# A six-stage decoder block on one core: the second cross attention issued in text order on four engines

## The chip, the cores and the metric

One core of a Trainium2 chip runs the whole program. The metric is device microseconds of one execution, a median over several. PE is TensorE's matmul, PEld its weight load, DVE is VectorE, ACT ScalarE, POOL GpSimd, SP SyncE, which here issues nearly all DMAs. `L1361` is line 1361 of the kernel before.

## The reference

Two layers on `x` of 4 batches x 256 tokens x 256 features, with a context of 1601 keys for each batch. Six stages add to `x`: self attention, a first cross attention to the context ("memory attention"), a ternary feed forward, a recurrence, the second cross attention, and a mixture of 8 experts of which each token uses 2. Each stage starts from the layer norm of `x`. The change is about the second cross attention and the experts, which share its time:

```python
q = _rms_norm((x @ Wq.T).reshape(b, 256, 16, 128), q_norm_w)
kv_in = concatenate([context, x], axis=1)            # 1857 keys
k = _rms_norm((kv_in @ Wk.T).reshape(b, 1857, 4, 128), k_norm_w)
v = (kv_in @ Wv.T).reshape(b, 1857, 4, 128)
q, k = _rope(q, positions_of_queries), _rope(k, positions_of_keys)
k, v = repeat(k, 4), repeat(v, 4)                    # 4 key heads serve 16 query heads
attn = softmax(q @ k.T / sqrt(128)) @ v
x = x + attn.reshape(b, 256, 2048) @ Wo.T

logits = layernorm(x) @ w_gate                       # 8 experts, the best 2 weighted
x = x + sum(weight * (silu(y @ wi_0[e]) * (y @ wi_1[e])) @ wo[e])
```

## The kernel before

All matrices are float32. Keys are handled in 15 chunks of 128 (the last has 65). A *head* is one of the 16 combinations of batch `b` and key head `g`; each has two *pairs* of query heads, so 32 pairs. A pair is worked through in 8 *steps* of two chunks:

- `score` (L1361 to L1366): on PE scores of a chunk for 512 queries (two heads x 256), `bsc`; ACT copies them, scaled by the key's factor `kn`, into a tile `s` of the ring of 12; DVE keeps the running maximum `acc`. ACT and DVE read the same PSUM bank, and DVE waits for ACT's copy.
- `maximum` (L1373 to L1379): after the last chunk PE transposes `acc` (`tm`), DVE reduces it to `mq`, and a half step or more later PE spreads `mq` over all partitions (`bc`).
- `exponential` (L1383 to L1398), ten steps after the score (`DE`): DVE subtracts `bc`, ACT takes the exponential, POOL adds the two halves to the row sums `sum`.
- `weigh` (L1407), eleven steps after the score (`DW`): PE multiplies by the values into `bpo`.
- `finish` (L1413 to L1441): ACT copies `bpo` to `aT`, PE adds up the sums over keys (`ts`), DVE inverts them, PE projects with `wo` (`bpw`), DVE adds the result to `x`.

`steps` (L1531) runs step `s` as: exponential of chunk pair `s-10`, score `s`, `others(2s)`, weigh `s-11`, `others(2s+1)`. The table `places` holds, for each *place* (half step), pieces of generators that prepare other work: `put(place, gen, last, bank)` enters one piece, and with `bank` moves on to the next place if the place already holds a piece that wants a bank. While head `k-1` is scored, from place `base = 32 (k-1)` on, head `k` is prepared:

- `prep_q` (L1229): `pq` on PE, ACT's squares, DVE's two products with cosine and sine tables (`rotate`), POOL's addition and its power -1/2 of the sum of squares (`factor`, L1196 to L1199), all in one piece; five places later ACT scales by the factor (`normed`, L1203); eight places after the first piece PE transposes (`tpq`) and ACT copies to `qT`.
- `prep_kv` (L1258), four units `i` of up to four chunks, at places 22, 26, 30 and 34 of `base`: projection `pk`, rotate and factor in one piece, eight places later the transposes `tpk` and ACT's copy to `kT` (L1303).
- for the first head of a batch also `angles` (nine pieces on DVE, the last with two sines on ACT, L1142 to L1144), `tokens` (layer norm of `x`, inverse root by `rsqrt`, whose power runs on POOL at L272) and `tables` (L1160 to L1165: four products on DVE for the keys, four for the queries, two to a piece; the keys' at places 7 and 11 of `base`).
- `tiles` (L1205), called by the first preparation, also issues the four loads of the values that the start of the program left in DRAM.

`experts(b)` of an earlier batch goes through the same table, in 23 pieces: seven of routing, then for each expert one piece of `mph` on PE, tanh on ACT and two products on DVE, and one of `mpe` on PE and DVE's addition to `x`. Three experts of batch 2 are kept for the end (`KEPT`), beside batch 3's.

PSUM tiles come from `p1`, a ring of six banks; `bc` and `bpo` have one each. SBUF tiles of 128x1024 for context, expert weights and raw keys come from `db`, three buffers.

The text only fixes dependencies and a priority: the framework's scheduler, which works with its own estimates of durations, puts the instructions of each engine into a fixed order, and each engine then runs its list in that order. The lists of all engines, SP's included, are made that way before. The first eight steps are entered while the last stages of batch 3 are still going; `run(work)` (L1596) enters all later ones.

Of the kernel before, what the change touches and what calls it, by code (L numbers as in the profile page):

```python
# [20 lines left out]
P = 128  # L21
# [95 lines left out]
def decoder_kernel(ctx: ExitStack, tc: tile.TileContext, at, t, out):  # L117
# [861 lines left out]
    def experts(b):  # L979
# [13 lines left out]
        r1 = rsqrt(mv[:, :, 1], 1e-5, f"mo{b}")  # L993
# [31 lines left out]
        V.tensor_sub(w2, tops[1], tops[0])  # L1025
        A.activation(w2, w2, AF.Exp)
# [13 lines left out]
        def inner(e):  # L1040
# [17 lines left out]
            A.activation(it, ph[:, 0:256], AF.Tanh, scale=0.5)  # L1058
            V.scalar_tensor_tensor(it, it, 1.0, ph[:, 0:256], ALU.add, ALU.mult)
# [18 lines left out]
        for e in range(NE + ahead):  # L1078
            if e < NE:
                its.append(inner(e))  # L1080
                if not final:
                    yield
            if e >= ahead:
                outer(e - ahead, its[e - ahead])
            yield
# [61 lines left out]

    def tables(b, only="kq"):

        d = bt[b]  # L1150
        ang, sn = d["angles"]
        for nm, n, w in (("k", NCH, knw), ("q", 2, qnw)):
            if nm not in only:
                continue
            tb = [P, n, 64]
            ctab = wk.tile([P, n, HD1], F32, tag=f"c{nm}", name=f"ctab{nm}{b}")
            stab = wk.tile([P, n, HD1], F32, tag=f"s{nm}", name=f"stab{nm}{b}")
            wlo, whi = w[:, None, 0:64].to_broadcast(tb), w[:, None, 64:128].to_broadcast(tb)
            d[nm] = (ctab, stab)
            V.tensor_mul(ctab[:, :, 0:64], ang[:, 0:n, :], wlo)  # L1160
            V.tensor_mul(ctab[:, :, 64:128], ang[:, 0:n, :], whi)
            yield

            V.scalar_tensor_tensor(stab[:, :, 64:128], sn[:, 0:n, :], -1.0, whi, ALU.mult, ALU.mult)
            V.tensor_mul(stab[:, :, 0:64], sn[:, 0:n, :], wlo)  # L1165
            yield

    def normed_tokens(b):
        mv = moments(xs[b], f"xb{b}")
        r1 = rsqrt(mv[:, :, 1], 1e-5, f"xb{b}")  # L1170
        bt[b]["centred"] = lambda: centred(fa(0, f"bxh{b}"), xs[b], mv, r1)
# [14 lines left out]
    def rotate(src, ctab, stab, sq, r, u):  # L1186


        A.activation(sq[:, :, 0:HD1], src, AF.Square)
        V.tensor_mul(r, src, ctab)  # L1190
        V.tensor_mul(u, src, stab)  # L1191
# [13 lines left out]
    def tiles(b, g):  # L1205

        if (b, g) not in gt:
# [11 lines left out]
            for i in range(4):  # L1219
                if (b, i) in kept_values:  # L1220
                    n, w = units(i)
                    r = min(P, w)
                    nc.sync.dma_start(
                        out=gt[b, g]["v"][0:r, 4 * i + 2 : 4 * i + 2 + n, :],
                        in_=kept_values[b, i][:, 0:r, g * HD1 : (g + 1) * HD1].rearrange("c p n -> p c n"),
                    )
        return gt[b, g]

    def prep_q(b, g, j):  # L1229
# [10 lines left out]
        ctab, stab = (a[:, j : j + 1, :].to_broadcast([P, 4, HD1]) for a in d["q"])  # L1240
# [3 lines left out]
        rotate(pq.rearrange("p (h d) -> p h d", h=4), ctab, stab, sq, r, u)  # L1244
        factor(sq, r, u, 4, nm, rn)
# [12 lines left out]
    def prep_kv(b, g, i):  # L1258
# [17 lines left out]
        if done:  # L1276
            o = n - done
            ctab, stab = (a[:, 4 * i + o : 4 * i + n, :] for a in d["k"])
            rotate(raw, ctab, stab, *(a[:, o:n, :] for a in (sq, r, u)))
        for h in range(0, n - done, 2):  # L1280
# [10 lines left out]
            ctab, stab = (a[:, 4 * i + h : 4 * i + h + m, :] for a in d["k"])  # L1291
# [4 lines left out]

        factor(sq, r, u, n, nm, e["kn"][:, 4 * i : 4 * i + n])
# [7 lines left out]
    def before_head(b, g):  # L1305

        if g == 0:
            if b == 0:
                yield from angles(b)
            yield from tables(b)  # L1310
        late = None
        for i in (1, 2, 3):
            gen = prep_kv(b, g, i)
            next(gen)
# [13 lines left out]
        for gen in (prep_q(b, g, 0), prep_q(b, g, 1), prep_kv(b, g, 0)):  # L1328
            next(gen)
# [125 lines left out]
    QA, KA, HB, HC = (2, 6), (11, 13, 15, 17), 5, 8  # L1455
# [37 lines left out]
    for k, (b, g) in enumerate(heads):  # L1493
        base = 32 * (k - 1)
        if k:
            if g == 0:
                gen = angles(b)
                for i in range(9):
                    put(base - 81 + 6 * i, gen, i == 8)
                gen = tokens(b)  # L1500
                for i, o in enumerate((-8, -6, -3)):
                    put(base + o, gen, i == 2, i == 2)
                for o, n in ((-5, "q"), (-3, "q"), (7, "k"), (11, "k")):
                    gen = tables(b, n) if o in (-5, 7) else gen
                    put(base + o, gen, o in (-3, 11))
            for f, when in ((prep_q, QA), (prep_kv, KA)):
                for i, o in enumerate(when):
                    gen = f(b, g, i)
                    spot = put(base + 2 * o, gen, bank=f is prep_q)
                    if f is prep_q:  # L1510
                        put(spot + HB, gen)
                    put(spot + HC, gen, True, True)
        gen = loader(b, g)
        put(base + 60, gen, True)
    for b in range(B - 1):
# [3 lines left out]
        pieces = 23 if b < B - 2 else 23 - 2 * KEPT  # L1519
        for i in range(pieces):  # L1520
            spot = put(spot, gen, i == 22, i not in (0, 1, 2, 5, 6)) + (5 if i > 6 else 3)
# [74 lines left out]
    run(work)  # L1596
    assert not places, sorted(places)
    gen = experts(B - 1)
    for _ in range(KEPT):
        next(gen)  # L1600
        next(kept)
        next(kept)
# [67 lines left out]
```

## Time and profile before

| what | value |
|---|---|
| median of 3 runs (lowest to highest) | 1747.34 us (1746.52 to 1749.41) |
| profiled execution, device time | 1749.43 us |
| its span, first to last instruction | 1747.4 us |
| mean granted TensorE clock | 0.993 |
| first score to last weighing | about 510 to 1709 us |
| POOL `sum` (L1398), 411 | 536.7 us, 1306 ns each |
| PE `bsc` (L1361) and `bpo` (L1407), 960 each | 459.5 and 459.9 us |
| ACT `s` (L1362), 480; `s` (L1386), 256 | 316.5 and 256.5 us |
| DVE `acc` (L1366), 448; `s` (L1383), 256 | 333.0 and 289.4 us |

A float32 matmul stands in the profile as two PE instructions, so a chunk's score of 128x512 counts two. Where a row of a group says `idle before <- releaser`, the engine stood still before these instructions and the releaser is what it waited for. In a list by order of time, the columns are start, duration from the first to the end of the last, engine, line, operation and tiles, how many are merged, and in brackets idle time before it. In a list by stretches, the columns are the stretch, its length, the busy time of each engine, the granted clock, the DMA share and GB/s.

### The profile page before, as it was taken

What the parts mean: (1) busy time and instruction counts of PE and PEld (TensorE: products, weight loads), DVE (VectorE), ACT (ScalarE), POOL (GpSimd) and SP (SyncE); (2) the same over time, 40 slices, a digit from 0 to 9 for tenths busy, and PEclk for the clock granted to TensorE, in tenths of its full rate; (3) what the DMA queues carried; (4) which work ended last, traced back from release to release, by engine and by line L of the source; (5) the groups of instructions that cost most, each with busy time, mean ns of one, the idle gap of its engine ahead of it and who ended that gap; (6) DMA issues with size and microseconds to landing.
All of it is one profiled execution on the core that took longest, in us unless ns stands there. A gap on an engine that the chain in (4) does not pass through costs nothing.

```text
span 1747.4 us, 20643 instructions
## 1 busy us (share of the span) xinstructions
PE 1694.9 (97%) x6642; PEld 971.5 (56%) x6642; DVE 1302.7 (75%) x2429; ACT 997.4 (57%) x1742; POOL 877.5 (50%) x719
## 2 busy tenths in 40 slices
PE   8899989999999999999999999999999999999998
PEld 4455668765555455554555555555555555445546
DVE  6653476787668777787877878777877878788776
ACT  3456653656456656566665656556565656656551
POOL 2210032211126576676766756655665776676651
PEclk9999999999999999999999999999999999999999
DMA  7221334212231121121212121121222113011102
GB/s 258 99 90 50 90 99 128 75 66 90 97 109 46 38 82 35 55 58 31 89 32 70 47 67 52 55 82 35 73 61 67 51 37 93 26 37 48 43 0 67
DMA packets 113554, 119.10 MB, mean 68 GB/s; under 512 B 10000, under 2 KB 87332, under 8 KB 113448
## 3 DMA queue, kind: packets, MB, share of 16 engines
q1 hardware_dynamic: 111624, 116.39, 21.6%
q10 hardware_dynamic: 1824, 1.41, 0.3%
q8 instruction: 53, 0.87, 0.2%
q14 instruction: 53, 0.43, 0.1%
HBM read 100.20 MB, written 17.57 MB: 67 GB/s over the span
## 4 chain that ended last, share of the span: by engine, by line
PE 64%; DVE 12%; POOL 9%; ACT 9%; issue 4%; DMA 1%; POOLq 0%; DVEq 0%; ACTq 0%
PE bpo L1407 17%; PE bsc L1361 16%; PE pk L1290 5%; POOL sum L1398 5%; PE mph L1053 2%; PE bpw L1437 2%; PE vah L355 2%; ACT s L1386 2%; ACT s L1362 2%; DVE acc L1366 1%; PE xpo L740 1%; DVE s L1383 1%; PE pq L1239 1%; POOL ropeq L1196 1%; PE xsc L695 1%
## 5 line engine op out<-in xcount | busy, mean ns | idle before, releaser
L1398 POOL TENSOR_TENSOR sum<-sum,s 128x512 f32<-128x512 f32 (+1 forms) x411 | 536.7, 1306 | 84.1 <-ACT s L1386 59.0
L1361 PE MATMUL bsc<-qTb,kTb 128*128 128x512 f32 (+1 forms) x960 | 459.5, 599 | 6.8 <-ACT kTb L1303 6.7
L1407 PE MATMUL bpo<-s,vb 128*128 128x512 f32 (+1 forms) x960 | 459.9, 598 | 0.4 <-ACT s L1386 0.4
L1362 ACT ACTIVATE s<-bsc,kn 128x512 f32<-128x512 f32 (+1 forms) x480 | 316.5, 683 | 211.6 <-PE bsc L1361 194.6
L1366 DVE SCALAR_TENSOR_TENSOR acc<-bsc,kn,acc 128x512 f32<-128x512 f32 x448 | 333.0, 743 | 89.2 <-ACT s L1362 73.3
L1383 DVE TENSOR_TENSOR s<-s,bc 128x1024 f32<-128x1024 f32 (+1 forms) x256 | 289.4, 1142 | 14.7 <-PE bc L1379 14.5
L1386 ACT ACTIVATE s<-s 128x1024 f32<-128x1024 f32 (+1 forms) x256 | 256.5, 1006 | 53.8 <-DVE s L1383 52.2
L1361 PEld LDWEIGHTS bsc<-qTb,kTb 128*128 128x128 f32 (+1 forms) x960 | 174.2, 188 | 191.9 <-issue 135.3
L1407 PEld LDWEIGHTS bpo<-s,vb 128*128 128x128 f32 (+1 forms) x960 | 169.8, 191 | 141.7 <-issue 137.9
L1389 POOL TENSOR_TENSOR sum<-s 128x512 f32<-128x512 f32 x32 | 40.8, 1276 | 198.6 <-ACT s L1386 198.6
L1196 POOL TENSOR_TENSOR ropek<-ropek,ropuk 128x512 f32<-128x512 f32 (+1 forms) x64 | 78.2, 1222 | 123.7 <-DVE ropuk L1191 122.4
L1203 ACT ACTIVATE ropeq<-ropeq,rnq 128x128 f32<-128x128 f32 x128 | 41.2, 390 | 110.7 <-POOL rnq L1199 107.1
L355 PE MATMUL vah<-wv,vcT 128*128 128x512 f32 (+1 forms) x156 | 77.7, 633 | 5.1 <-DMA vcT<-in_ctxT 3.1
L1290 PEld LDWEIGHTS pk<-wkv,cTk 128*128 128x128 f32 x624 | 76.3, 192 | 8.3 <-issue 4.5
L1290 PE MATMUL pk<-wkv,cTk 128*128 128x128 f32 x624 | 77.4, 275 | 0.0
L1199 POOL TENSOR_TENSOR kn<-ssk,nhalf 128x4 f32<-128x4 f32 (+1 forms) x64 | 66.2, 1034 | 17.5 <-DVE ssk L1198 15.0
L1364 DVE TENSOR_SCALAR acc<-bsc,kn 128x512 f32<-128x512 f32 x32 | 24.0, 750 | 59.7 <-ACT s L1362 59.7
L1437 PEld LDWEIGHTS bpw<-wo,aT 128*128 128x128 f32 x256 | 48.5, 190 | 34.8 <-issue 21.1
L272 POOL TENSOR_TENSOR rsr_xa<-rse_xa,nhalf 128x2 f32<-128x2 f32 x4 | 3.4, 854 | 126.0 <-DVE rse_xa L270 126.0
L1437 PE MATMUL bpw<-wo,aT 128*128 128x256 f32 x256 | 65.6, 379 | 0.3 <-ACT aT L1413 0.3
L1196 POOL TENSOR_TENSOR ropeq<-ropeq,ropuq 128x512 f32<-128x512 f32 x32 | 43.8, 1368 | 40.2 <-PE bsc L1361 17.8
L358 ACT COPY vst<-vah 128x512 f32<-128x512 f32 (+1 forms) x52 | 30.2, 591 | 56.0 <-issue 18.3
(509 smaller groups left out, 2589.7 us busy)
## 6 DMA issues: line engine op xcount, KB each, us to landing
v<-vst SPq DMA_DIRECT2D x48, 256.0 KB
vb<-v SPq DMA_DIRECT2D x48, 256.0 KB
cTk<-in_ctxT SPq DMA_DIRECT2D x24, 512.0 KB
wq<-in_wq SPq DMA_DIRECT2D x16, 512.0 KB
wo<-in_wo SPq DMA_DIRECT2D x16, 512.0 KB
wi<-in_wi SPq DMA_DIRECT2D x32, 256.0 KB
xcT<-in_ctxT SPq DMA_DIRECT2D x12, 512.0 KB
xct<-in_ctx SPq DMA_DIRECT2D x12, 512.0 KB
```

The lines of the kernel that those rows point to most:

```text
L355: T.matmul(pv[0:r, :], lhsT=cT[:, c, k * P : k * P + r], rhs=wv[c], start=c == 0, stop=c == 1)
L1196: G.tensor_tensor(r4, r4, u4[:, :, ::-1, :], ALU.add)
L1199: G.tensor_tensor(rn, ss[:, 0:n], nhalf[:, 0:n], ALU.pow)
L1290: T.matmul(pk[:, q, 0:w], lhsT=src, rhs=e["wkv"][:, c, 0:w], start=c == 0, stop=c == 1)
L1361: T.matmul(pc[0:n, :], lhsT=e["kT"][:, k * P : k * P + n], rhs=q, start=True, stop=True)
L1362: A.activation(s[0:n, i, :], pc[0:n, :], AF.Copy, scale=e["kn"][0:n, k : k + 1])
L1366: V.scalar_tensor_tensor(self.acc[0:n, :], pc[0:n, :], e["kn"][0:n, k : k + 1], self.acc[0:n, :], ALU.mult, ALU.max)
L1383: V.tensor_tensor(s[0:n, 0:w, :], s[0:n, 0:w, :], self.bc[0:n, None, :].to_broadcast([n, w, 512]), ALU.subtract)
L1386: A.activation(s[0:n, 0:w, :], s[0:n, 0:w, :], AF.Exp)
L1398: G.tensor_tensor(self.sum[0:n, :], self.sum[0:n, :], s[0:n, i, :], ALU.add)
L1407: T.matmul(self.po, lhsT=e["v"][0:n, k, :], rhs=self.s[c][0:n, i, :], start=k == 0, stop=k == NCH - 1)
L1437: T.matmul(pw[:, j * 256 : j * 256 + 256], lhsT=aT[:, o : o + P], rhs=e["wo"][:, self.h + h, :], start=True, stop=True)
```

## The change

- `run(work)` stands in `tc.manual_schedule` for PE, DVE, ACT and POOL: from the ninth step on, their instructions keep the order of the text. SP's list is still the scheduler's.
- Pieces are divided. `prep_q` and `prep_kv` yield between `rotate` and `factor`, so POOL's part comes two places after DVE's. A query goes at 0, +2, +6 and +9 places; key units go in the order 1, 2, 0, 3 at places 14, 18, 23, 27, with +2 and +7. An expert is three pieces (PE and ACT; DVE; PE and DVE) with 2, 3 and 5 places between, and routing one piece more: 32 in all.
- The values' loads are a generator of their own, at place 22 of `base`.
- Keys' tables: `tables_ahead` makes the four quarters ahead, one every five places from -29 on, each in a `db` tile that SP stores to DRAM; `load_tables` at place 3 loads all four. The tables' shape is now [P, 2, n, 64], one half after the other, and `rotate` reads them through a four-dimensional pattern.
- `root`, an addition and three Newton steps on DVE (`newton`, the helper that the self attention uses), takes the place of `rsqrt` for batches 1 to 3 in `normed_tokens` and for batches 0 to 2 in `experts`.
- `before_head` follows the new yields and loads the values itself.

```diff
@@ -990,7 +990,7 @@
...
         yield
-        r1 = rsqrt(mv[:, :, 1], 1e-5, f"mo{b}")
+        r1 = rsqrt(mv[:, :, 1], 1e-5, f"mo{b}") if final else root(mv, f"mo{b}")
         yield
@@ -1023,6 +1023,7 @@
...
         V.tensor_sub(w2, tops[1], tops[0])
+        yield
         A.activation(w2, w2, AF.Exp)
@@ -1056,6 +1057,8 @@
...
             A.activation(it, ph[:, 0:256], AF.Tanh, scale=0.5)
+            if not final:
+                yield
             V.scalar_tensor_tensor(it, it, 1.0, ph[:, 0:256], ALU.add, ALU.mult)
@@ -1077,7 +1080,7 @@
...
             if e < NE:
-                its.append(inner(e))
+                its.append((yield from inner(e)))
                 if not final:
@@ -1145,29 +1148,65 @@
...
+    def new_tables(b, nm):
+        n = NCH if nm == "k" else 2
+        bt[b][nm] = tuple(wk.tile([P, 2, n, 64], F32, tag=f"{c}{nm}", name=f"{c}tab{nm}{b}") for c in "cs")
+        return bt[b][nm]
+    def quarter(b, nm, i, dst):
+        n, w = (NCH, knw) if nm == "k" else (2, qnw)
+        src = bt[b]["angles"][i // 2][:, 0:n, :]
+        k = 1 - i % 2 if i > 1 else i % 2
+        w = w[:, None, 64 * k : 64 * k + 64].to_broadcast([P, n, 64])
+        if i == 3:
+            V.tensor_mul(dst, src, w)
+        elif i == 2:
+            V.scalar_tensor_tensor(dst, src, -1.0, w, ALU.mult, ALU.mult)
+        else:
+            V.tensor_mul(dst, src, w)
     def tables(b, only="kq"):
-        d = bt[b]
-        ang, sn = d["angles"]
-        for nm, n, w in (("k", NCH, knw), ("q", 2, qnw)):
-            if nm not in only:
-                continue
-            tb = [P, n, 64]
-            ctab = wk.tile([P, n, HD1], F32, tag=f"c{nm}", name=f"ctab{nm}{b}")
-            stab = wk.tile([P, n, HD1], F32, tag=f"s{nm}", name=f"stab{nm}{b}")
-            wlo, whi = w[:, None, 0:64].to_broadcast(tb), w[:, None, 64:128].to_broadcast(tb)
-            d[nm] = (ctab, stab)
-            V.tensor_mul(ctab[:, :, 0:64], ang[:, 0:n, :], wlo)
-            V.tensor_mul(ctab[:, :, 64:128], ang[:, 0:n, :], whi)
-            yield
-
-            V.scalar_tensor_tensor(stab[:, :, 64:128], sn[:, 0:n, :], -1.0, whi, ALU.mult, ALU.mult)
-            V.tensor_mul(stab[:, :, 0:64], sn[:, 0:n, :], wlo)
-            yield
+        for nm in only:
+            tabs = new_tables(b, nm)
+            for i in range(4):
+                quarter(b, nm, i, tabs[i // 2][:, (1 - i % 2) if i > 1 else i % 2])
+                if i % 2:
+                    yield
+    kept_tables = {}
+    def tables_ahead(b):
+        kept_tables[b] = []
+        for i in range(4):
+            w = db(f"tab{b}{i}")[:, 0 : NCH * 64]
+            quarter(b, "k", i, w.rearrange("p (n d) -> p n d", n=NCH))
+            d = dram.tile([P, NCH * 64], F32, tag=f"t{b}{i}", name=f"t{b}{i}")
+            nc.sync.dma_start(out=d, in_=w)
+            kept_tables[b].append(d)
+            yield
+    def load_tables(b):
+        tabs = new_tables(b, "k")
+        for i, d in enumerate(kept_tables[b]):
+            nc.sync.dma_start(
+                out=tabs[i // 2][:, (1 - i % 2) if i > 1 else i % 2].rearrange("p n d -> p (n d)"), in_=d
+            )
+        yield
+    def root(mv, nm):
+        v = sm([P, 2], "rse2", f"rse_{nm}")
+        V.tensor_scalar(v, mv[:, :, 1], 1e-5, None, ALU.add)
+        return newton(v, nm, 2)
...
         mv = moments(xs[b], f"xb{b}")
-        r1 = rsqrt(mv[:, :, 1], 1e-5, f"xb{b}")
+        r1 = root(mv, f"xb{b}") if b else rsqrt(mv[:, :, 1], 1e-5, f"xb{b}")
         bt[b]["centred"] = lambda: centred(fa(0, f"bxh{b}"), xs[b], mv, r1)
@@ -1187,8 +1226,9 @@
         A.activation(sq[:, :, 0:HD1], src, AF.Square)
-        V.tensor_mul(r, src, ctab)
-        V.tensor_mul(u, src, stab)
+        src4, r4, u4 = (a.rearrange("p n (h d) -> p n h d", h=2) for a in (src, r, u))
+        V.tensor_mul(r4, src4, ctab)
+        V.tensor_mul(u4, src4, stab)
@@ -1216,15 +1256,17 @@
...
             }
-            for i in range(4):
-                if (b, i) in kept_values:
-                    n, w = units(i)
-                    r = min(P, w)
-                    nc.sync.dma_start(
-                        out=gt[b, g]["v"][0:r, 4 * i + 2 : 4 * i + 2 + n, :],
-                        in_=kept_values[b, i][:, 0:r, g * HD1 : (g + 1) * HD1].rearrange("c p n -> p c n"),
-                    )
         return gt[b, g]
+    def load_values(b, g):
+        for i in range(4):
+            n, w = units(i)
+            r = min(P, w)
+            nc.sync.dma_start(
+                out=tiles(b, g)["v"][0:r, 4 * i + 2 : 4 * i + 2 + n, :],
+                in_=kept_values[b, i][:, 0:r, g * HD1 : (g + 1) * HD1].rearrange("c p n -> p c n"),
+            )
+        yield
@@ -1237,11 +1279,14 @@
...
             T.matmul(pq, lhsT=d["yT"][:, c, j * P : (j + 1) * P], rhs=e["wq"][:, c, :], start=c == 0, stop=c == 1)
-        ctab, stab = (a[:, j : j + 1, :].to_broadcast([P, 4, HD1]) for a in d["q"])
+        ctab, stab = (
+            a[:, :, j : j + 1, :].rearrange("p h n d -> p n h d").to_broadcast([P, 4, 2, 64]) for a in d["q"]
+        )
...
         rotate(pq.rearrange("p (h d) -> p h d", h=4), ctab, stab, sq, r, u)
+        yield
         factor(sq, r, u, 4, nm, rn)
@@ -1275,7 +1320,7 @@
...
             o = n - done
-            ctab, stab = (a[:, 4 * i + o : 4 * i + n, :] for a in d["k"])
+            ctab, stab = (a[:, :, 4 * i + o : 4 * i + n, :].rearrange("p h n d -> p n h d") for a in d["k"])
             rotate(raw, ctab, stab, *(a[:, o:n, :] for a in (sq, r, u)))
@@ -1288,12 +1333,13 @@
...
                     T.matmul(pk[:, q, 0:w], lhsT=src, rhs=e["wkv"][:, c, 0:w], start=c == 0, stop=c == 1)
-            ctab, stab = (a[:, 4 * i + h : 4 * i + h + m, :] for a in d["k"])
+            ctab, stab = (a[:, :, 4 * i + h : 4 * i + h + m, :].rearrange("p h n d -> p n h d") for a in d["k"])
             rotate(pk[:, 0:m, 0:HD1], ctab, stab, *(a[:, h : h + m, :] for a in (sq, r, u)))
...
+        yield
         factor(sq, r, u, n, nm, e["kn"][:, 4 * i : 4 * i + n])
@@ -1308,9 +1354,11 @@
...
             yield from tables(b)
+        run(load_values(b, g))
         late = None
...
             gen = prep_kv(b, g, i)
+            next(gen)
             next(gen)
@@ -1326,6 +1374,7 @@
...
         for gen in (prep_q(b, g, 0), prep_q(b, g, 1), prep_kv(b, g, 0)):
+            next(gen)
             next(gen)
@@ -1452,7 +1501,7 @@
-    QA, KA, HB, HC = (2, 6), (11, 13, 15, 17), 5, 8
+    QA, KA, HB, HC, HQ = (4, 12), ((1, 14), (2, 18), (0, 23), (3, 27)), 6, 7, 9
     DE, DW = 10, 11
@@ -1494,31 +1543,41 @@
...
             if g == 0:
+                gen = tokens(b)
+                for i, o in enumerate((-8, -6, -3)):
+                    put(base + o, gen, i == 2, i == 2)
                 gen = angles(b)
...
                     put(base - 81 + 6 * i, gen, i == 8)
-                gen = tokens(b)
-                for i, o in enumerate((-8, -6, -3)):
-                    put(base + o, gen, i == 2, i == 2)
-                for o, n in ((-5, "q"), (-3, "q"), (7, "k"), (11, "k")):
-                    gen = tables(b, n) if o in (-5, 7) else gen
-                    put(base + o, gen, o in (-3, 11))
-            for f, when in ((prep_q, QA), (prep_kv, KA)):
-                for i, o in enumerate(when):
-                    gen = f(b, g, i)
-                    spot = put(base + 2 * o, gen, bank=f is prep_q)
-                    if f is prep_q:
-                        put(spot + HB, gen)
-                    put(spot + HC, gen, True, True)
+                gen = tables_ahead(b)
+                for i in range(4):
+                    put(base - 29 + 5 * i, gen, i == 3)
+                gen = tables(b, "q")
+                for i in range(2):
+                    put(base - 5 + 3 * i, gen, i == 1)
+                put(base + 3, load_tables(b), True)
+            for i, o in enumerate(QA):
+                gen = prep_q(b, g, i)
+                spot = put(base + o, gen, bank=True)
+                put(spot + 2, gen)
+                put(spot + HB, gen)
+                put(spot + HQ, gen, True, True)
+            for i, o in KA:
+                gen = prep_kv(b, g, i)
+                put(base + o, gen)
+                put(base + o + 2, gen)
+                put(base + o + HC, gen, True, True)
+            put(base + 22, load_values(b, g), True)
         gen = loader(b, g)
...
-        pieces = 23 if b < B - 2 else 23 - 2 * KEPT
+        pieces = 32 if b < B - 2 else 32 - 3 * KEPT
         for i in range(pieces):
-            spot = put(spot, gen, i == 22, i not in (0, 1, 2, 5, 6)) + (5 if i > 6 else 3)
+            now, wait = (i not in (0, 1, 2, 5, 6, 7), 3) if i < 8 else ((True, 2), (False, 3), (True, 5))[(i - 8) % 3]
+            spot = put(spot, gen, i == 31, now) + wait
     kept = gen
@@ -1593,13 +1652,14 @@
...
     run(first)
-    run(work)
+    with tc.manual_schedule(engines=set(ENGINES)):
+        run(work)
     assert not places, sorted(places)
...
         next(gen)
-        next(kept)
-        next(kept)
+        for _ in range(3):
+            next(kept)
     run(kept)
```

## The prediction

> **What bounds the kernel now.** I read the page from its top, then the waits of PE, then the order of time round the longest wait, then the clock of the same stretches.
>
> ```profile
> PE 1694.9 (97%) x6642; PEld 971.5 (56%) x6642; DVE 1302.7 (75%) x2429; ACT 997.4 (57%) x1742; POOL 877.5 (50%) x719
> PE 64%; DVE 12%; POOL 9%; ACT 9%; issue 4%; DMA 1%; POOLq 0%; DVEq 0%; ACTq 0%
> ```
>
> PE is busy 97% of the span and two thirds of the chain that ended last. The change removes no matmul, so it can only win what PE loses by waiting. In the second cross attention (553 to 1690 us, before the drain) the waits of PE are:
>
> ```profile
> PE bc L1379 <- DVE mq L1375: 6.9, 3, 2.5
> PE bsc L1361 <- ACT kTb L1303: 6.7, 10, 1.2
> PE tpk L1301 <- DVE it L1060: 3.0, 5, 0.7
> PE tm L1373 <- DVE acc L1366: 2.3, 1, 2.3
> PE bpo L1407 <- ACT s L1386: 0.4, 1, 0.4
> ```
>
> Columns: total us, times, longest. That is 19.3 us in 20 waits. The view counts from the modelled end of the matmul before; a 128x512 matmul lasts 0.59 but the next starts 0.43 after it (four take 1.72 from start to start), so each wait costs some 0.16 more: 3.2 us.
>
> What the worst of them looks like, in order of time:
>
> ```profile
> 739.44 9.15 POOL L1398 TENSOR_TENSOR sum<-sum,s 128x512 f32<-128x512 f32 x6 [0.53 <-ACT s L1386]
> 749.77 1.01 POOL L1199 TENSOR_TENSOR rnq<-ssq,nhalf 128x4 f32<-128x4 f32 x1
> 750.82 1.28 ACT L1203 ACTIVATE ropeq<-ropeq,rnq 128x128 f32<-128x128 f32 x4 [6.07 <-POOL rnq L1199]
> 752.70 0.75 DVE L1364 TENSOR_SCALAR acc<-bsc,kn 128x512 f32<-128x512 f32 x1 [5.23 <-ACT s L1362]
> 753.37 0.68 DVE L1375 TENSOR_REDUCE mq<-tm 128x4 f32<-128x512 f32 x1
> 754.10 0.65 PE L1379 MATMUL bc<-cst,mq 128*128 128x128 f32 x4 [2.26 <-DVE mq L1375]
> ```
>
> POOL had 9.15 us of row sums queued; the factor of a query's RoPE (L1199) stood behind them, ACT stood on that factor for 6.07 us, DVE on ACT's score copies for 5.23, PE on DVE's reduction for 2.26. No engine was short of time: a queue head waited for something planned too early. The clock answers:
>
> ```profile
> 748.00:760.00 12.00, 9.74 (x25) 4.27 (x25) 7.26 (x11) 4.95 (x10) 4.03 (x4) 0.86 0.00 0
> 1056.00:1068.00 12.00, 9.55 (x25) 4.66 (x24) 8.36 (x12) 5.22 (x11) 3.23 (x3) 0.86 0.00 0
> 1371.00:1383.00 12.00, 9.85 (x32) 4.93 (x31) 8.89 (x14) 6.81 (x13) 5.65 (x5) 1.00 0.10 31
> 1544.00:1556.00 12.00, 9.66 (x29) 5.02 (x28) 9.28 (x16) 4.90 (x8) 10.08 (x9) 0.86 0.29 90
> ```
>
> The column 0.86 is the granted clock: after three of the four long waits 12 us ran at 0.86, 1.7 us lost each, 5.0 in all. Together PE can win 19.3 + 3.2 + 5.0 = 27.5 us here.
>
> [...]
>
> **The change, part by part.** *Text order on PE, ACT, DVE and POOL.* First, is any engine over-full? For each pair of heads (8 steps) I added count times mean duration in the order of the built programs (two matmuls of 0.43 for each 128x512, score copy 0.68, maximum 0.74, subtraction 1.21, exponential 1.06, POOL sum 1.31 twice, and so on). Before, DVE is over PE where the key tables and angles fall: pair 6 has 37.2 us of DVE against 36.5 of PE, pair 14 41.1 against 40.8, pair 22 40.2 against 39.9. After, PE leads in every pair from 1 to 30 (closest: pair 10 with 35.9 against 36.9, pair 27 with 33.7 against 35.0). The work of a pair no longer bunches.
>
> Second, does the in-order chain fit? With PE's score at 0, a bare step is 1.72 of scores and 1.72 of weighing. ACT's two copies end at 2.65, DVE's second maximum at 3.4 (it waits for ACT's copy of the same bank; the group of L1366 is 73.3 us idle on L1362), the next step's subtraction at 4.6, its exponential at 5.7; weighing needs it at 8.6. Cover 2.9 us. Queued behind a late subtraction are ACT's exponential and copies, then PE. The query factor now stands 4 half steps (some 8.6 us) ahead of ACT's use, and POOL has at most 2.6 + 2.6 + 2.5 us of work between, so the 6.07 us wait has no cause left. I take all 27.5 as won. Bounds: nothing (every wait comes back elsewhere) to 27.5.
>
> *The key copy at a head's start.* Keys' unit 0 is transposed in the last half step of a head (half step 30 is taken by a finish, so 31). In the new order of PE, 14 of the 15 transposes are followed at once by the new head's first score, which reads the copy; before, weighing (0.86 or 1.72 us) stood between. From the rows of one such transpose before, printed after this paragraph, the last of the four starts 0.33 after 707.11, the copy ends at 708.33 and a score could start 0.07 later: 708.41 - 707.44 - 0.11 (the next start anyway) = 0.86 us. 14 x 0.86 = +12.0. Bounds: 0, if another instruction hides it, to 14 x 1.45, if a score copy (0.68) is still ahead on ACT.
>
> ```profile
> 707.11 0.60 PE L1301 MATMUL tpk<-cst,ropek 128*128 128x128 f32 x4
> 707.75 0.58 ACT L1303 COPY kTb<-tpk 128x512 f32<-128x512 f32 x1 [1.71 <-PE tpk L1301]
> ```
>
> *Inverse square roots from POOL to DVE* (six: `normed_tokens` of batches 1 to 3, `experts` of 0 to 2). Removed: one POOL power (0.5 to 2.1 us, L272); added: 11 small DVE operations for it, in one piece of 12 with the addition. In the experts' case the piece stands behind a query's two table products (0.68 each, ready at 4.9) and ahead of the next subtraction: 4.9 + 12 x 0.17 + 1.21 + 1.06 + 0.3 of handovers = 9.5; weighing needs it after steps of 4.3 and 3.4 us and 1.72 of scores = 9.4. Late 0.1 to 0.2, three times: +0.6. In the tokens' case the steps are 4.5 and 5.6, cover 2.6. The 0.17 is an operation on a few columns with POOL still (L1029 to L1036, 0.13 to 0.18); the same lines show 0.69, 1.10 and 1.18 with a POOL sum running. Bounds for the mean of the 12: 0.17 and 0.9. I take 0.17, because POOL's next sum waits for the exponential behind this very piece, so POOL has run dry.
>
> [...]
>
> *Key tables through DRAM.* The same four products (1.6 + 1.7 + 1.4 + 1.5 us) leave the head's start and stand one in 2.5 steps; added on SP are 3 x (4 stores, 4 loads) of 0.49 MB. The four loads are issued 11 half steps (over 20 us) ahead of their first reader; at the 248 GB/s of the page's first slices (258) 1.97 MB take 8 us. Behind them on SP stand `wo`, `wq` and the next context tile, due a head later. Each table borrows one of three `db` buffers, so a context tile may start late: 0 to 2 us, three times; I take 0, since SP's order has those tiles ahead of the last store. Values loaded at half step 22: the tile is free only then; a wait on SP goes away, not on PE.
>
> *Sine block* (unchanged, now fixed): 1.00 + 1.00 + 1.09 + two table loads of 1.28 = 5.7 us on ACT; exponential at 9.4, needed at 4.5 + 5.6 + 1.72 = 11.8. Hidden; without that cover 2.4 more would be needed before it costs. *Experts in 32 pieces:* same operations, a bank held a step longer; five waits of `tpk` on it (3.0 us) are in the 27.5.
>
> *The drain.* The order before filled the time between the last `bc` and the final pair's weighing with the sums and projections; in text order only one matmul pair (0.86) stands there: 1.21 + 1.06 + 0.3 - 0.86 = +1.7.
>
> Sum: -27.5 + 12.0 + 0.6 + 1.7 = -13.2. The profiled execution took 1749.4 (span 1747.4, 2.0 round it), so 1736.2 for such a one; it lies 2.1 over the median of 1747.3, hence **1734.1** for the median.
>
> **Rivals.** *A, the key copy is hidden:* 1747.3 - 27.5 + 1.7 = 1721.5. For it: before, a single weighing of 0.86 was enough in the rows above (score at 708.41, just behind the copy). Against: now nothing stands between on PE; that ACT is free at 6.4 (exponential 5.7, one copy 0.68) while the transposes end at 7.6 (3.44 + 0.86 + 0.86 + 1.72 + 0.44 + 0.27) only keeps the price from growing. *B, no net change:* one more wait as long as the key copy's at each head (the maximum's transposes `tm` have only 1.7 us of cover, against DVE's pieces up to 1.5), 14 x 0.9 more: 1747. *C, slower:* the square roots on DVE contend with POOL. At a mean of 0.45 us for the 12, each experts' piece is 12 x 0.28 + 0.2 = 3.6 late and each tokens' piece 0.8; three of them also draw the low clock (1.7): 10.8 + 2.4 + 5.1 = 18.3, less the 0.6 already counted: 1751.8. It decides from a mean of 0.37 on, where its 13 us eat the gain. For: 1.10 and 1.18 in the rows, and two such operations (1539 to 1541 us) stand shortly ahead of the 2.3 us wait on `acc`. Against: POOL dry there.
>
> **How the numbers follow.** Forecast 0.46, A 0.18, B 0.13, C 0.23. About 0.2% (3.5 us) is what a measurement here can tell from no change. Faster: the forecast nearly whole plus A, 0.63; same: B and the forecast's edge, 0.14; slower: C, 0.23. The forecast's own range is 1727 to 1742 (the key copy's price from 0.4 to 1.4 each). The range 1717 to 1756 reaches under A by the context tiles' and handovers' few us, and over C by a mean of 0.5.
>
> **What would show it.** Right: no wait of `bc` on `mq`, clock 1.00 from 553 us on, ACT's `ropeq` (110.7 us idle before it now) nearly without waits on `rnq`, and 14 waits of `bsc` on `kTb` of 0.7 to 0.9. Wrong: PE waiting for exponentials two steps after a square root, DVE operations of two columns at 0.5 us and more, or a wait of `pk` on a DMA.

## The result: 2031.4 us, 16% slower

The changed kernel takes 2031.37 us (median of 4 runs, 2028.76 to 2032.77) against 1747.9 (median of 4 in the same job, 1746.52 to 1749.41): 1.162 times as long, 95% interval 1.16 to 1.164, or 283.5 us more. The forecast was 1734.1, the range ended at 1756, and no rival was near.

Page of the changed kernel (span 2027.0 us): its engines, and the chain of work that ended last.

```profile
PE 1785.3 (88%) x6642; PEld 996.7 (49%) x6642; DVE 1325.1 (65%) x2495; ACT 988.1 (49%) x1743; POOL 857.1 (42%) x713
DVE 4%; PE 3%; issue 1%; ACT 1%; DMA 0%; SPq 0%; DVEq 0%; ACTq 0%
```

PE does the same 6642 instructions but is idle 2027.0 - 1785.3 = 241.7 us instead of 52.5 (+189), and its busy time is 90 us longer, at most 71 of it by the lower granted clock (mean 0.959 against 0.993; last section). 189 + 90 is the difference of the spans. The chain ends after a few per cent here, so it says nothing. The waits of all engines do (engine and line, what it waited for: total us, times, longest):

```profile
ACT s L1435 <- DVE s L1432: 671.8, 242, 6.3
POOL sum L1447 <- ACT s L1435: 513.7, 207, 6.7
DVE acc L1415 <- ACT s L1411: 371.8, 220, 4.8
POOL sum L1438 <- ACT s L1435: 141.2, 32, 6.0
DVE acc L1413 <- ACT s L1411: 51.6, 31, 1.7
```

The same two waits before:

```profile
DVE acc L1366 <- ACT s L1362: 73.3, 66, 4.3
ACT s L1386 <- DVE s L1383: 52.2, 68, 2.6
```

So ACT's exponential waited in 68 of its 256 places for DVE's subtraction and now waits in 242. DVE's `acc` waited in 66 of 448 for ACT's copy and now waits in 220, that is once in nearly every step of two chunks: ACT waits for DVE and DVE for ACT. PE's own waits from 553 to 1950 us:

```profile
PE bsc L1410 <- ACT kTb L1349: 47.7, 16, 4.3
PE bpo L1456 <- ACT s L1435: 32.7, 27, 3.5
PE bsc L1410 <- DVE acc L1415: 32.7, 14, 4.8
PE bpo L1456 <- ACT aT L1462: 17.7, 9, 3.8
PE pk L1335 <- DVE acc L1415: 17.6, 10, 3.6
```

PE waits for whatever ACT or DVE do last: copies, maxima, exponentials. That is no single late producer; two engines as a whole are late. One step in order of time (start, duration, engine, line, operation; in brackets the idle time of the engine before it and what ended it):

```profile
1005.48 1.21 DVE L1432 TENSOR_TENSOR s<-s,bc 128x1024 f32<-128x1024 f32 x1
...
1006.73 1.06 ACT L1435 ACTIVATE s<-s 128x1024 f32<-128x1024 f32 x1 [4.10 <-DVE s L1432]
1007.69 1.25 ACT L1411 ACTIVATE s<-bsc,kn 128x512 f32<-128x512 f32 x2
...
1008.39 1.60 DVE L1415 SCALAR_TENSOR_TENSOR acc<-bsc,kn,acc 128x512 f32<-128x512 f32 x2 [1.70 <-ACT s L1411]
...
1009.91 0.41 DVE L1230 TENSOR_TENSOR ropek<-pk,ctabk 128x256 f32<-128x256 f32 x1
1010.24 0.41 DVE L1231 TENSOR_TENSOR ropuk<-pk,stabk 128x256 f32<-128x256 f32 x1
...
1012.05 1.21 DVE L1432 TENSOR_TENSOR s<-s,bc 128x1024 f32<-128x1024 f32 x1
...
1013.30 1.06 ACT L1435 ACTIVATE s<-s 128x1024 f32<-128x1024 f32 x1 [1.95 <-DVE s L1432]
```

This is a loop through two queues. DVE subtracts (1.21 us); ACT's exponential waits for that; ACT's score copies stand behind the exponential in the text; DVE's first maximum waits for the copy of the same PSUM bank (1.70 us here); and DVE's next subtraction stands behind the second maximum. From the subtraction to the end of the maxima it is 1005.48 to 1009.99 = 4.51 us if no other piece stands between (a bare step), of which DVE stands still 1.70. No data run round this loop: text order makes it, by setting the exponential ahead of copies that it has nothing to do with. Every further DVE piece, such as the RoPE products, lengthens it (here the next subtraction starts at 1012.05).

So the time of a pair (8 steps, from one `tm` to the next) should be DVE's busy time plus 8 x 1.70 = 13.6 us, and that is nearly what the trace of the changed kernel gives, added up from its records:

| stretch, by the pair whose `tm` ends it (from 0) | DVE busy, us | + 13.6 | measured |
|---|---|---|---|
| 8 (little prepared) | 23.5 | 37.1 | 36.7 |
| 27 (keys of the next head) | 36.2 | 49.8 | 51.9 |
| 21 (keys, tokens, experts) | 39.8 | 53.4 | 57.3 |
| all 31 stretches | 950.0 | 1371.6 | 1425.2 |

The rule gives 96% of the time; before, the same 31 stretches took 1153.5 us. The waits listed above agree with it: DVE's maxima stood 371.8 + 51.6 = 423.4 us on ACT's copies, and 31 x 13.6 is 421.6.

### The profile page after: what moved, and what is told of

It reads as the page before. It is cut to its first block, busy times and chain, and to the rows that moved or that the text cites. A ratio compares the mean times of both kernels' runs of the same rounds, so it can differ in the third digit from the quotient of the medians.

```text
span 2027.0 us, 20768 instructions
## 1 busy us (share of the span) xinstructions
PE 1785.3 (88%) x6642; PEld 996.7 (49%) x6642; DVE 1325.1 (65%) x2495; ACT 988.1 (49%) x1743; POOL 857.1 (42%) x713
## 5 line engine op out<-in xcount | busy, mean ns | idle before, releaser
L1447 POOL TENSOR_TENSOR sum<-sum,s 128x512 f32<-128x512 f32 (+1 forms) x411 | 522.6, 1272 | 531.7 <-ACT s L1435 513.7
L1415 DVE SCALAR_TENSOR_TENSOR acc<-bsc,kn,acc 128x512 f32<-128x512 f32 x448 | 336.0, 750 | 395.2 <-ACT s L1411 371.8
L1435 ACT ACTIVATE s<-s 128x1024 f32<-128x1024 f32 (+1 forms) x256 | 256.7, 1003 | 672.2 <-DVE s L1432 671.8
L1410 PE MATMUL bsc<-qTb,kTb 128*128 128x512 f32 (+1 forms) x960 | 487.2, 626 | 82.5 <-ACT kTb L1349 47.7
L1456 PE MATMUL bpo<-s,vb 128*128 128x512 f32 (+1 forms) x960 | 490.2, 633 | 57.6 <-ACT s L1435 37.6
L1411 ACT ACTIVATE s<-bsc,kn 128x512 f32<-128x512 f32 (+1 forms) x480 | 302.4, 673 | 7.5 <-PE bsc L1410 6.7
L1456 PEld LDWEIGHTS bpo<-s,vb 128*128 128x128 f32 (+1 forms) x960 | 180.5, 202 | 247.8 <-issue 148.4
L1335 PE MATMUL pk<-wkv,cTk 128*128 128x128 f32 x624 | 85.7, 289 | 35.8 <-DVE acc L1415 17.6
L1335 PEld LDWEIGHTS pk<-wkv,cTk 128*128 128x128 f32 x624 | 81.2, 201 | 51.0 <-DVE acc L1415 22.1
L1486 PEld LDWEIGHTS bpw<-wo,aT 128*128 128x128 f32 x256 | 48.7, 191 | 36.3 <-issue 23.5
L1054 PE MATMUL mph<-yTm,wi 128*128 128x256 f32 x256 | 60.9, 382 | 6.4 <-DVE acc L1415 6.4
L1281 PE MATMUL pq<-wq,yTb 128*128 128x512 f32 x128 | 60.2, 593 | 0.0
L1054 PEld LDWEIGHTS mph<-yTm,wi 128*128 128x128 f32 x256 | 48.1, 190 | 23.8 <-DVE acc L1415 11.5
```

What stands on the lines that cost most here:

```text
L1054: T.matmul(ph[:, i * 256 : i * 256 + 256], lhsT=wi[:, i, c, e % 2 * ME : (e % 2 + 1) * ME], rhs=yT[:, c, :], start=c == 0, stop=c == 1,)
L1335: T.matmul(pk[:, q, 0:w], lhsT=src, rhs=e["wkv"][:, c, 0:w], start=c == 0, stop=c == 1)
L1410: T.matmul(pc[0:n, :], lhsT=e["kT"][:, k * P : k * P + n], rhs=q, start=True, stop=True)
L1411: A.activation(s[0:n, i, :], pc[0:n, :], AF.Copy, scale=e["kn"][0:n, k : k + 1])
L1415: V.scalar_tensor_tensor(self.acc[0:n, :], pc[0:n, :], e["kn"][0:n, k : k + 1], self.acc[0:n, :], ALU.mult, ALU.max)
L1435: A.activation(s[0:n, 0:w, :], s[0:n, 0:w, :], AF.Exp)
```

## The experiments

All change the order or place of work, none what is computed. Theory L is the loop just shown.

**1. The exponential behind the copies.** In the changed kernel, text order kept; ACT's exponential and POOL's sums move behind the score.

```diff
+            yield
             A.activation(s[0:n, 0:w, :], s[0:n, 0:w, :], AF.Exp)
...
-                pairs[m].exponential(i)
+            ex = pairs[m].exponential(i) if 0 <= m < len(pairs) else iter(())
+            next(ex, None)
             if n < len(pairs):
                 pairs[n].score(c)
+            run(ex)
```

> The exponential and its sums move behind the score's two copies and maxima in the text; the subtraction stays ahead of them. Theory L (loop): in text order DVE's subtraction, ACT's exponential, ACT's two copies behind it, DVE's maximum behind those copies and the next subtraction form a ring of 1.21 + 1.06 + 0.68 + 0.68 + 0.75 = 4.4 us plus five handovers, into which every other piece on DVE or ACT is added; the median distance of two exponentials was 5.6 us with the change and 4.6 on average before. With the exponential behind the copies the ring takes two steps, PE sets the pace again: 1735 to 1770 us. Theory R (the roots on DVE, contention with POOL, the key copies): none of that is touched, 1990 to 2040 us.

Measured: 1784.11 us, ratio to before 1.02 (1.018 to 1.022; before 1747.63 in this job). This edit takes back 247 of 283 us, with all else as in the change; theory L's range ended at 1770, so 14 us or more of the cost lie elsewhere (numbers 5 and 6 find some). The two waits of the loop, 671.8 and 371.8 us in the changed kernel, are now:

```profile
ACT s L1436 <- DVE s L1432: 134.2, 92, 4.9
DVE acc L1415 <- ACT s L1411: 60.0, 59, 3.5
```

**2. The maximum ahead of the copy.** The loop opened at another place: in `score` DVE's maximum precedes ACT's copy.

```diff
-                A.activation(s[0:n, i, :], pc[0:n, :], AF.Copy, scale=e["kn"][0:n, k : k + 1])
                 if k == 0:
...
+                A.activation(s[0:n, i, :], pc[0:n, :], AF.Copy, scale=e["kn"][0:n, k : k + 1])
```

> In the score DVE's maximum comes ahead of ACT's copy of the same bank; the exponential stays ahead of both. Theory L: DVE no longer waits for ACT's copies, so the ring is open although the exponential still stands ahead of the copies: 1735 to 1780 us, and the idle time of DVE ahead of the maximum that ends on ACT's copy (371.8 us) is nearly gone. Theory R: 1990 to 2040 us.

Measured: 1806.04 us, 1.0324 (1.0308 to 1.034), 26 us over the end of theory L's range. Of the 423.4 us that DVE's maxima waited for ACT's copies no wait is left in the list, while ACT still waits for the subtraction:

```profile
ACT s L1435 <- DVE s L1432: 405.2, 227, 6.1
```

Cutting another link of the same loop takes back 225 us, so it is the loop and not the exponential's place as such.

**3. The scheduler's order, and 4. text order alone.** Number 3 is the change without the manual order, number 4 the kernel before with nothing but the manual order.

```diff
# 3, in the changed kernel
-    with tc.manual_schedule(engines=set(ENGINES)):
-        run(work)
+    run(work)
# 4, in the kernel before
-    run(work)
+    with tc.manual_schedule(engines=set(ENGINES)):
+        run(work)
```

> The changed kernel without the manual schedule: the order is the scheduler's again, all divided pieces, roots and tables stay. Theory L: 1735 to 1765 us, since the scheduler places subtractions ahead of the maxima when they are ready. A theory T, that the new places, the roots or the table transfers cost the time, expects 1950 us or more.

> The kernel before with the manual schedule and nothing else. Theory L: the ring is in its text too, so 1990 to 2120 us (the undivided pieces of the old places add to the ring, and the query factor's wait on POOL stays). Theory T (the new pieces are the cause, text order is harmless): below 1800 us.

Measured: number 3 1773.82 us, 1.0137 (1.0111 to 1.0163); number 4 2012.5 us, 1.1508 (1.1483 to 1.1532). Text order alone costs 265 us on the old pieces, and its waits are those of the change:

```profile
ACT s L1386 <- DVE s L1383: 679.2, 246, 5.4
...
DVE acc L1366 <- ACT s L1362: 367.1, 220, 4.9
```

The same sum fits it: DVE busy 946.9 + 31 x 13.6 = 1368.5 us against 1409.1 measured. Number 3 is 9 us over theory L's range: the change's pieces cost 26 us even in the scheduler's order, and why was not taken apart.

**5. The first key unit two places earlier**, on top of number 1:

```diff
-    QA, KA, HB, HC, HQ = (4, 12), ((1, 14), (2, 18), (0, 23), (3, 27)), 6, 7, 9
+    QA, KA, HB, HC, HQ = (4, 12), ((1, 14), (2, 18), (0, 21), (3, 27)), 6, 7, 9
```

> The changed kernel with the exponential split (1784.1 us) and, on top, the pieces of each head's first key unit two places earlier (21, 23 and 28 of the head before in place of 23, 25 and 30), so that two whole weighings and a score stand between the key transposes and the first score of the next head. Theory K (the first score waits for ACT's copy of the key transposes, a latency that this order leaves open): the 15 waits bsc <- ACT kTb of 18.7 us go, and most of the 19.4 us lost between tpk and bsc in the stretch 553 to 1690 us: 1765 to 1773 us. Rival Q (the copy is late because ACT's queue is late as a whole at that point, behind the exponential): the wait moves to the next reader of ACT, bpo <- ACT s grows by about as much: 1779 to 1785 us.

Measured: 1752.59 us, 1.0031 (1.002 to 1.0043; before 1746.83), 31 us less than number 1 and 12 better than expected. PE's waits from 553 to 1710 us, number 1 and then number 5:

```profile
PE bsc L1410 <- ACT kTb L1349: 18.7, 15, 1.9
PE bpo L1457 <- ACT s L1436: 15.8, 14, 2.8
```

```profile
PE bpo L1457 <- ACT s L1436: 13.9, 14, 1.9
PE bsc L1410 <- DVE acc L1415: 2.4, 4, 0.7
```

The waits for the key copy are gone and did not move to the exponentials, so theory K holds. Of the 31 us, the loss between transposes and score accounts for 19.4; the rest, of which 2.3 lie before the first maximum, is spread over pairs and was not taken apart.

**6. The six roots back on POOL**, on number 1 (`rsqrt` in place of `root` in `normed_tokens` and `experts`).

```diff
-        r1 = rsqrt(mv[:, :, 1], 1e-5, f"mo{b}") if final else root(mv, f"mo{b}")
+        r1 = rsqrt(mv[:, :, 1], 1e-5, f"mo{b}")
...
-        r1 = root(mv, f"xb{b}") if b else rsqrt(mv[:, :, 1], 1e-5, f"xb{b}")
+        r1 = rsqrt(mv[:, :, 1], 1e-5, f"xb{b}")
```

> The changed kernel with the exponential split (1784.1 us), and the six reciprocal roots of the four-engine stretch back on POOL (rsqrt with a power, as before) in place of twelve small DVE operations each. Rival C of the prediction (small DVE operations held up by POOL, DVE late for ACT and PE) expects a gain of 5 us or more: 1770 to 1779 us. Theory L (once the exponential is out of the ring, DVE has room: the trace shows most of the twelve operations at 0.16 to 0.17 us, about 3 us for a root) expects 1781 to 1786 us: the gain of the shorter DVE chain is spent waiting for POOL, whose queue holds two sums of 2.6 us per step.

Measured: 1767.55 us, 1.0115 (1.0098 to 1.0132): 16.5 us less than number 1. Theory L's figure fell; rival C's gain of 5 us or more came, and 2.5 us more than its range allowed. Between the two profiled spans (17.2 us apart) 5.6 arise before the first maximum, where nothing was edited, so only the 11.6 behind it can be put down to the roots; the pairs in which the tokens are normed (5, 13, 21) give 3.1, 4.8 and 3.2. One of these in number 1, in order of time:

```profile
1010.70 2.61 POOL L1448 TENSOR_TENSOR sum<-sum,s 128x512 f32<-128x512 f32 x2 [4.34 <-ACT s L1436]
...
1012.51 0.82 DVE L1204 TENSOR_SCALAR rse_xb<-mv_xb 128x2 f32<-128x2 f32 x1
1013.26 1.26 POOL L1236 TENSOR_TENSOR ropek<-ropek,ropuk 128x512 f32<-128x512 f32 x1
1013.37 1.19 DVE L279 TENSOR_SCALAR nr_xb<-rse_xb 128x2 int32<-128x2 int32 x1
1014.59 0.17 DVE L280 TENSOR_SCALAR nr_xb<-nr_xb 128x2 int32<-128x2 int32 x1
```

Operations on two columns last 0.82 and 1.19 us and end with POOL's (1013.31 and 1014.52); the next takes 0.17. A root of the tokens took 4.01 us there instead of 2.4.

**7. The old pieces with the same split.** Number 4 with the edit of number 1.

> The kernel before with text order alone (2012.5 us), and the exponential split so that ACT's exponential and POOL's sums stand behind the score's copies. Theory L (the ring subtraction, exponential, copy, maximum is what text order costs, whatever the pieces): at least 220 of the 265 us go: 1765 to 1795 us, near the changed kernel with the same split (1784.1). Rival P (the old pieces, which hold an operation and its reader in one place, are what text order cannot bear, so that the change's division is needed): 1830 us or more.

Measured: 1782.36 us, 1.0203 (1.0187 to 1.0218): 230 of 265 us gone, and level with number 1. In text order with this split, the division of the pieces, the new places, the roots and the tables together brought nothing over the old ones.

**8. Both openings at once.** Number 5 with the edit of number 2.

> As the kernel with the split and the earlier first key unit, and in the score DVE's maximum ahead of ACT's copy in the text. Theory L: the ring is open already, so that the second opening is worth little, and ACT's copies now start 0.75 us later behind each maximum, which the exponential behind them passes on: within 8 us of the kernel without it, and rather slower than faster. Rival (the remaining waits bpo <- ACT s and bsc <- DVE acc come from DVE's late maximum, which waits for ACT): 10 us or more faster.

Measured: 1902.45 us, 1.0887 (1.0846 to 1.0928): 150 us slower than number 5. Both theories missed. Waits over the whole span:

```profile
ACT s L1415 <- DVE acc L1414: 443.7, 227, 6.3
...
PEld bpo L1457 <- ACT s L1436: 128.3, 68, 5.8
PE bpo L1457 <- ACT s L1436: 102.6, 58, 5.5
...
DVE ropek L1230 <- ACT squares L1228: 98.2, 59, 4.3
```

The exponential now stands in ACT's list behind copies that wait for both maxima, so DVE's pieces delay the exponentials, and PE waits for them 58 times. DVE also waits for ACT's squares, 98.2 us against 43.8 in number 5: this looks like a loop of its own (maxima, copies, exponential, squares, RoPE products, next maxima), but nothing separated it.

**9 to 12. Three edits together**, and from there one step each: 9 is the split, the key unit and POOL's roots; 10 ends the manual order at the last score; 11 makes the key tables in place again; 12 gives number 9 to the scheduler.

```diff
# 10
     with tc.manual_schedule(engines=set(ENGINES)):
-        run(work)
+        while step < NPAIR * len(pairs):
+            step = next(work) + 1
+    run(work)
# 11
-                gen = tables_ahead(b)
...
+                gen = tables(b, "k")
+                for i in range(2):
+                    put(base + 7 + 4 * i, gen, i == 1)
...
-                put(base + 3, load_tables(b), True)
```

> The changed kernel with three edits: the exponential split, the first key unit two places earlier (these two: 1752.6 us) and the six roots back on POOL (worth 16.5 us on the split alone). If the three costs lie at different places and add: 1736 us, under the kernel before (1746.8). If the root's cost lay in the waits that the key edit has already removed (the token chain feeds the first key unit): 1748 to 1753 us.

> As the kernel with the three edits, with the manual order ended at the last score, so that the scheduler orders the steps behind it. From the last score to the last weighing the kernel with the split and the key edit takes 31.1 us, the kernel before 23.9. Theory D (text order spaces the last exponentials out behind pieces that no longer have a score to fill the step): 4 to 7 us faster than the kernel with the three edits. Rival (the spacing is that of exponential, sums and weighing themselves): within 2 us.

> As the kernel with the three edits, with the keys' tables made in place in two pieces at places 7 and 11 of each batch's first head, as before, and no copies through DRAM. Prediction's step: tables through DRAM cost 0 (0 to 2 us three times), so this is within 3 us. Rival T (two products of 960 columns in one piece make DVE late by 2.3 us or more three times over): 4 to 10 us slower than the kernel with the three edits.

> As the kernel with the three edits, in the scheduler's order instead of text order (the exponential is in two parts in the text). Scheduler order of the unedited change: 1773.8 us, of which the roots are worth up to 16.5: 1755 to 1770 us. If so, text order with an open ring is worth 15 us or more over the scheduler's on these pieces, which is what the change was after. Rival (the pieces, not the order, set the time once the ring is open): within 5 us of the kernel with the three edits.

| kernel | us | ratio to before (1746.34) |
|---|---|---|
| 9 three edits | 1745.44 | 0.9993 (0.9982 to 1.0004) |
| 10 last steps to the scheduler | 1740.01 | 0.9951 (0.9933 to 0.997) |
| 11 key tables in place | 1747.25 | 0.9999 (0.9989 to 1.001) |
| 12 all by the scheduler | 1763.13 | 1.0093 (1.0076 to 1.011) |

Number 9 lies between its two expectations: the roots are worth 7.2 us here against 16.5 on number 1. Of the 9 us less, 5.6 are the part of number 6 that arose before the first maximum; behind it the profiled executions differ by 8.9 us here and 11.6 there, and whether the difference had sat in waits that the key edit removed is not shown. In 10, last score to last weighing takes 24.5 us instead of 29.5, and the whole is 5.4 us faster: theory D holds. In 11 the intervals overlap, so that the 1.8 us between the tables' two ways can't be told from nothing. 12 against 9 says that on the same pieces the open text order beats the scheduler's by 17.7 us. Number 10 is faster than the kernel before by 0.5%, a gain that the interval just sets apart from none. Its page:

```profile
PE 1693.0 (97%) x6642; PEld 973.5 (56%) x6642; DVE 1331.4 (77%) x2429; ACT 1022.7 (59%) x1743; POOL 868.7 (50%) x719
```

## Why the prediction was wrong, point by point

- **The step that failed is "does the in-order chain fit?"** It let ACT's copies end at 2.65 and DVE's second maximum at 3.4, as if ACT were free for them; the exponential of the same step stands ahead of them in the text and was left out. It then compared one pass (subtraction at 4.6, exponential at 5.7) with PE's need at 8.6 and called 2.9 us a cover. But the maximum that ends the pass starts the next one. As a loop it took 4.51 us a step in the changed kernel's trace, against the 3.44 (1.72 + 1.72) of PE's bare step, and cutting one link took back 247 of the 283 us (number 1). Every link was in the text of the prediction, the wait of maximum on copy included.
- **The load table was set against the wrong limit.** It showed DVE below PE in every pair from 1 to 30, by as little as 1.0 us, and DVE's busy time is indeed below PE's in all 31 stretches of the changed kernel's trace (PE's at a granted clock of 0.95 from 553 to 1950 us). But in the loop DVE cannot work 1.70 us of each step. The prediction's own durations give nearly this time: while ACT does the exponential (1.06) and the first copy (0.68), 1.74 in all, DVE waits. With 1.70, the profile of before would have told that text order is dear: its DVE busy time in the 31 stretches is 921.6 us, plus 31 x 13.6 = 1343 against the 1153.5 that they took, some 190 us slower.
- **27.5 us of waits, all won:** the waits named did go (in the changed kernel no `bc` on `mq`, and ACT's `ropeq` on `rnq` 2.7 us instead of 107.1), but in the changed kernel the loop put others in their place. Even with the loop open and the key waits gone (number 9) PE waits 17.2 us from 553 to 1710, 13.0 of them in 13 waits for exponentials, against the 19.3 of before: what the term counted as won came back at other places.
- **Clock 1.00 from 553 us on:** 0.95 for 553 to 1950 in the changed kernel.
- **Key copy, 14 x 0.86 = 12.0:** right in kind (15 waits in number 1), under-sized: 1.25 us each in the waits, 19.4 us between transposes and score, and 31 when the whole unit was moved. In the changed kernel itself the loop made them 3.0 each (47.7 in 16).
- **Roots, +0.6:** in the changed kernel the mean of the small operations is 0.166 us, as taken, with POOL idle beside all but the first of each tokens' root (0.26); but 12 of them, 2.3 to 2.4 us, stand in the loop. Once the loop is open POOL runs beside the first two of a tokens' root (0.82 and 1.19 us in number 6's rows), and the roots cost 7 to 12 us. Rival C had this, at 18.3 too dear, and it was not what made the kernel slow (number 4 has no such roots and takes 2012.5 us); its place was half right: the long operations are in the tokens' roots, none in the experts'.
- **Key tables, 0:** number 11 agrees, as far as 1.8 us can be told. **Drain, +1.7:** 31.1 us against 23.9 in number 5, and 5.4 to be had back (number 10); the step counted one link and not the spacing of the last exponentials.
- **No rival was the loop.** All three priced single late instructions; the slow one ended at 1752.

Open: what else the new pieces cost in the scheduler's order (number 12 is still 16.8 us above before), and the 150 us of number 8.

## What to carry to other kernels

When several engines run one hand-written order, look for loops through their queues: follow each wait to its engine's previous instruction in the list until you are back where you began one step later. The loop's length is the least time of a step, and the idle time that it forces on an engine must be added to that engine's load before loads are compared. Put an instruction that nobody needs soon behind those that another engine waits for, and try one opening at a time: of the two here, each of which took back over 220 us, the second on top of the first cost 150 us (number 8 against number 5).

## What the runs showed of the hardware that was not expected

**Slow matmuls behind a wait of 1.92 us.** Number 5, PE in order of time, and the clock of two stretches (the figure ahead of the DMA share):

```profile
932.65 3.43 PE L1457 MATMUL bpo<-s,vb 128*128 128x512 f32 x4 [1.92 <-ACT s L1436]
```

```profile
928.00:932.00 4.00, 2.74 (x9) 1.22 (x7) 3.86 (x12) 1.03 (x2) 1.66 (x2) 1.00 0.02 6
932.00:936.00 4.00, 3.35 (x5) 1.42 (x6) 3.90 (x8) 2.71 (x4) 3.18 (x3) 0.63 0.45 125
```

Four weighings take 3.43 us, at a granted clock of 0.63 from 932 to 936 us, where four at a clock of 1.00 in the kernel before (737.50 us) last 3 x 0.43 + 0.59 = 1.88. No length of wait from which the clock falls is shown: before, it was 1.00 for the 12 us that hold a wait of 2.2 us (1371 to 1383). In the changed kernel, with PE idle 241.7 us against 52.5, such stretches are frequent: of the 116 windows of 12 us from 553 to 1945 us, 32 have a clock under 0.90 (before, 2 of the 94 from 553 to 1681); the two below show 0.84 and 0.78. Its mean granted clock is 0.959 against 0.993 before, which is (1 - 0.959) x 2027.0 - (1 - 0.993) x 1747.4 = 71 us more lost to the clock; at most so much of the 90 us of longer busy time is the clock's, and the rest was not taken apart.

```profile
1015.00:1027.00 12.00, 7.19 (x25) 4.03 (x24) 6.93 (x15) 9.39 (x13) 6.77 (x6) 0.84 0.07 23
1027.00:1039.00 12.00, 9.61 (x22) 4.25 (x21) 7.81 (x16) 4.83 (x7) 6.87 (x6) 0.78 0.13 44
```

**A DVE operation with one input lasted longer beside POOL as well.** L1204 and L279 in number 6's rows have a single SBUF input and took 0.82 and 1.19 us, ending with POOL's operations; the prediction took a mean of 0.17. In the changed kernel, where POOL has just ended when L279 starts, L279 takes 0.17. In the kernel before, L1029 (one input, two columns) lasted 0.75 us at 909.22 with POOL's sums running and 0.16 at 1725.74 with POOL idle. Not every one does: L1030, the reciprocal behind it, took 0.15 at 914.49 with the sums running.
